# A two-layer Toeplitz mixer on Trainium2: the buffer of q * v packed densely, small tables loaded through GpSimd's queue, and the second layer's matrices written later

## The chip, the cores and the metric

The kernel runs on one core of one Trainium2 chip. The metric is device time in microseconds (us), lower is better. Before the change three runs took 6179.19, 6186.65 and 6196.39 us; the median is 6186.65 us. One further execution was taken with the hardware profiler; it took 6175.88 us, and every figure called "the trace" comes from it.

## The reference, cut to what matters

The whole network has four layers over an image batch of 8 x 56 x 56 x 192. The change touches only what the first two, of one kind, share. Each of these two computes, for every sample and channel (D1 is 576),

```
q = silu(x @ q_w.T + q_b);  v = silu(x @ v_w.T + v_b);  p = silu(x @ p_w.T + p_b)
decay = sl ** distance                        # per channel, sl from the layer's slope
a1, a2 = mlp(position) * decay                # two tables of 111 numbers per channel
qv = q * v
o1 = toeplitz along the image's width  of qv with a1
o2 = toeplitz along the image's height of qv with a2
out = (p * (o1 + o2)) @ o_w.T + o_b           # x = x + out
```

A Toeplitz product of length 56 is a multiplication by a 56 x 56 matrix whose rows are shifted copies of the table, one such matrix for each channel and direction.

## The kernel before, in words

All of it is float32. The work of the first two layers goes through four kinds of steps, and memory on the chip's outside (HBM) carries the data between them.

**q * v (`tno_qv`, lines 218 to 357).** Tiles of 128 tokens of two pairs of samples are multiplied with the q and v weights (line 257; the first four tiles of the first layer at line 278), get a bias (266, 285), silu (295) and the product (298). Three transfers for each tile, for 8, 8 and 2 *half blocks* of 32 channels, write the product to `qv` on SyncE's queue (line 301). `qv` has 18 half blocks. Each holds 64 x 56 rows of 128 numbers, of which the image fills the first 56 x 56 (T is 3136); the last 8 x 56 rows are padding, which one transfer for each of the two buffers fills with zeros at the start (line 720, on GpSimd's queue).

**The tables (`decay_tables`, from line 129).** For each layer, 18 small loads (slope and MLP weights, lines 133 to 166), a small MLP on TensorE and VectorE, and ten stores of finished tables to HBM (line 193). All 28 transfers of a layer are on SyncE's queue. A buffer `a` of a table has two copies; GpSimd clears its last column (line 182) once the transfer before has landed.

**The matrices (`expand_tables`, line 195).** 36 transfers for each layer, HBM to HBM, write `mat` from the tables: each copies 64 x 32 runs of 56 numbers (224 bytes) that start one element apart (line 201). Both layers' matrices, 72 transfers, are made during the first q * v pass of layer 0.

**The Toeplitz products (`tno_toeplitz`, from line 359).** Nine blocks of 64 channels, and for each block two directions: 18 steps n in one stage. A step loads q (`load`) and its matrices into `tm` (line 382), multiplies (`along`, line 394), and turns the result back with transposes (`turned`, line 411). For direction d = 0, `load` issues two transfers of 56 x 56 runs of 512 bytes (line 372). For d = 1 it issues one transfer: 128 partitions of 28,672 bytes (line 375). The q tile has two buffers, and the load for step n + 2 is issued when `along` of step n is done. In `along` only rows 0 to 55 of each 64 are multiplied, so the eight padding rows are loaded and never used. Sums go to HBM from GpSimd's queue (line 427).

**The output projection (`tno_out`, from line 463)** loads the sums (line 487) and x (line 114) on SyncE's queue, gates them with p, projects, and stores x on GpSimd's queue (line 117).

`tno_layers` (from line 670) sets the order. `weave` runs one "lane" of q * v or projection steps and pulls steps from another generator between them. Lane 0 is the first q * v pass with the table and matrix work beside it; it is placed by a scheduler that orders every engine's instructions by estimated times. Lanes 1 to 4 each carry a Toeplitz stage (`TZ`) among their q * v and projection steps; there TensorE, ScalarE and VectorE keep the order in which they are written, and only the two queues of transfers (SyncE's and GpSimd's) are still placed by estimate. SyncE's queue is one sequence: a transfer whose wait isn't over holds up all behind it. In the built program each of its transfers also uses one of eight semaphores in turn, and waits for the transfer eight places before it to land; GpSimd's queue has eight of its own.

Of the kernel before, what the change touches and what calls it, by code (L numbers as in the profile page):

```python
# [12 lines left out]
F32 = mybir.dt.float32  # L13
# [8 lines left out]
B, H, W, C = 8, 56, 56, 192  # L22
T = H * W
# [3 lines left out]
D1 = 576  # L27
# [6 lines left out]
def view(ap, offset, dims):  # L34

    return bass.AP(ap.tensor, ap.offset + offset, [ap.ap[0], *dims])


class Net:
# [89 lines left out]
    def decay_tables(self, L, p, tables):  # L129

        nc, inp = self.nc, self.inp
        tv = p.tile([32, 111], F32, name="tv", bufs=1)
        nc.sync.dma_start(tv, inp["tvec"])
        pows = []
        for c in range(5):
            m = min(128, D1 - 128 * c)
            sl = p.tile([128, 1], F32, name="sl")
            nc.sync.dma_start(sl[:m], inp[f"{L}_slope"][128 * c : 128 * c + m, :])
            nc.vector.tensor_scalar(sl[:m], sl[:m], 0.0, 1.0, ALU.max, ALU.min)
            nc.vector.tensor_scalar(sl[:m], sl[:m], 1.0 - 0.95, 0.95, ALU.mult, ALU.add)  # L140
            pw = p.tile([128, 64], F32, name="pw", bufs=5)
            nc.gpsimd.memset(pw[:m, 0:1], 1.0)
            n = 1
            while n < 64:
                nc.vector.tensor_scalar(
                    pw[:m, n : 2 * n], pw[:m, 0:n], sl[:m], None, ALU.mult
                )
                n *= 2
                if n < 64:
                    sq = p.tile([128, 1], F32, name="sl")  # L150
                    nc.vector.tensor_mul(sq[:m], sl[:m], sl[:m])
                    sl = sq
            pows.append(pw)
        for d in range(2):
            t = f"{L}_t{d + 1}"
            w0 = p.tile([32, 2], F32, name="w0")
            nc.sync.dma_start(w0[:, 0:1], inp[f"{t}_w0"])
            nc.sync.dma_start(w0[:, 1:2], inp[f"{t}_b0"])
            ws = p.tile([32, 3, 32], F32, name="ws")
            nc.sync.dma_start(ws, inp[f"{t}_ws"])  # L160
            bs = p.tile([32, 3], F32, name="bs")
            nc.sync.dma_start(bs, inp[f"{t}_bs"])
            wo = p.tile([32, D1], F32, name="wo")
            nc.sync.dma_start(wo, inp[f"{t}_wo"])
            bo = p.tile([128, 5], F32, name="bo")
            nc.sync.dma_start(bo, inp[f"{t}_bo"])
            h = p.tile([32, 111], F32, name="h")
            nc.vector.tensor_scalar(h, tv, w0[:, 0:1], w0[:, 1:2], ALU.mult, ALU.add)
            nc.vector.tensor_scalar(h, h, 0.0, None, ALU.max)
            for i in range(3):  # L170
                hp = self.bank2()[:32, 0, :111]
                nc.tensor.matmul(hp, ws[:, i, :], h, start=True, stop=True)
                h = p.tile([32, 111], F32, name="h")
                nc.vector.tensor_scalar(h, hp, bs[:, i : i + 1], 0.0, ALU.add, ALU.max)
            for c in range(5):
                m = min(128, D1 - 128 * c)
                ap = self.bank2()[:, 0, :111]
                nc.tensor.matmul(
                    ap[:m], wo[:, 128 * c : 128 * c + m], h, start=True, stop=True
                )  # L180
                a = p.tile([128, 112], F32, name="a")
                nc.gpsimd.memset(a[:m, 111:112], 0.0)
                back = view(pows[c][:m], 55, [[-1, 55]])
                for lo, hi, dec in ((0, 55, back), (55, 111, pows[c][:m, 0:56])):
                    nc.vector.scalar_tensor_tensor(
                        view(a[:m], 110 - lo, [[-1, hi - lo]]),
                        ap[:m, lo:hi],
                        bo[:m, c : c + 1],
                        dec,
                        ALU.add,  # L190
                        ALU.mult,
                    )
                nc.sync.dma_start(tables[d][128 * c : 128 * c + m, :], a[:m])

    def expand_tables(self, tables, mats):

# [21 lines left out]
    def tno_qv(self, L, j0, xs, gn, qv, apart=None):  # L218
# [3 lines left out]
        nc, p, inp = self.nc, self.tp, self.inp  # L222
# [5 lines left out]
        w, bias = self.wq[:, 0:2], self.wq[:, 2]  # L228
# [62 lines left out]
        def multiply(m, n, z, at, c0):  # L291
            k = n // 128
            for f in stores:
                f()
            nc.scalar.activation(z[:m, :n, :], z[:m, :n, :], AF.Silu)  # L295
            prod = p.tile([128, 4, DC * 4], F32, name="t4")
            half = z[:m, :n, :].rearrange("p (n h c) b -> p n h (c b)", h=2, c=DC)
            nc.vector.tensor_mul(prod[:m, :k], half[:, :, 0], half[:, :, 1])  # L298
            n0 = c0 // 128
            stores[:] = [  # L300
                lambda: nc.sync.dma_start(
                    qv[2 * n0 : 2 * n0 + 2 * k, at : at + m, :].rearrange("n t e -> t n e"),
                    prod[:m, :k].rearrange("p n (h e) -> p (n h) e", h=2),
                )
            ]
# [7 lines left out]
        if apart:  # L313
            units = []
            for g in range(2):
                x, t0, n = loaded[g]
                for s in range(0, n, 128):
                    for c0 in range(0, 2 * D1, 512):
                        k = min(512, 2 * D1 - c0)
# [19 lines left out]
        for g in range(2 if apart else 0, groups):  # L339
            x, t0, n = loaded.pop(0)  # L340
            for s in range(0, n, 128):
                m = min(128, n - s)
                for c0 in range(0, 2 * D1, 512):
                    k = min(512, 2 * D1 - c0)
# [14 lines left out]
    def tno_toeplitz(self, j0, mats, qv, o):  # L359
# [3 lines left out]
        nc, p = self.nc, self.tz  # L363
        PR = H // 2

        def load(n):
            blk, d = divmod(n, 2)
            q = p.tile([128, H, 128], F32, name="q", bufs=2)
            if d == 0:
                for half in range(2):  # L370
                    of = qv[2 * blk + half, :T].rearrange("(h w) e -> w h e", w=W)
                    nc.sync.dma_start(q[64 * half : 64 * half + W], of)
            else:
                of = qv[2 * blk : 2 * blk + 2].rearrange("n (h w) e -> (n h) (w e)", w=W)
                nc.sync.dma_start(q.rearrange("p i e -> p (i e)"), of)
            return q

# [59 lines left out]
        for n in range(NS):  # L437
            blk, d = divmod(n, 2)
# [220 lines left out]
            pass  # L659

    @staticmethod
    def part(gen, t):

        for dt in gen:
            yield dt
            t -= dt
            if t <= 0:
                return

    def tno_layers(self, x0, x1, x2, gn, last):  # L670


        tc, nc = self.tc, self.nc
        LS = ("L0", "L1")
        tables = [

            [self.dram.tile([D1 + 1, 112], F32, name=f"{L}_tab{d}") for d in range(2)]
            for L in LS
        ]
# [3 lines left out]
        ]  # L683
        qvs = {

            j0: self.dram.tile([D1 // 32, 64 * W, 128], F32, name=f"qv{j0}") for j0 in (0, 2)
        }
        o = [self.dram.tile([B // 2, 9, 128, T], F32, name=f"{L}_sum") for L in LS]
        x = (x0, x1, x2)
        with ExitStack() as ctx, ExitStack() as wqp:  # L690
# [5 lines left out]
            QT, OT, TZT = 25 * 2.25 * 5.3, 28 * 10.7, 8 + 72 * 3.2  # L696

            with tc.tile_pool(name="tab", bufs=2) as tab:
                stats = [self.input_stats(x0, gn[0], j, tab) for j in range(4)]
                for more in stats[0]:  # L700
                    pass
                first = Q(0, 0, tab)
                next(first)

                for n in range(14):
                    next(first)
                    next(stats[1], None)
                for more in stats[1]:
                    pass
                for n in range(10):  # L710
                    next(first)
                self.decay_tables("L0", tab, tables[0])
                for st in stats[2:]:
                    for more in st:
                        next(first)
                none = tab.tile([112, 512], F32, name="none", bufs=1)
                nc.gpsimd.memset(none, 0.0)
                for qv in qvs.values():
                    to = qv[:, T:].rearrange("n (p k) e -> p n (k e)", p=112)
                    nc.gpsimd.dma_start(to, view(none, 0, [[0, D1 // 32], [1, 512]]))  # L720
                self.decay_tables("L1", tab, tables[1])
                for t in tables:
                    for d in range(2):
                        nc.gpsimd.dma_start(t[d][D1:], none[:1, :112])
                lanes = [[(first, QT - 104.0)], [(Q(0, 2), QT)], [(O(0, 0), OT), (Q(1, 0), QT)]]
                lanes += [[(O(0, 2), OT), (Q(1, 2), QT)], [(O(1, 0), OT)], [(O(1, 2, False), OT)]]
                mat = (m for i in range(2) for m in self.expand_tables(tables[i], mats[i]))
                self.weave(lanes[0], mat, lanes[1][0][0], 72.0, 0.0, 0.88)
            in_order = tc.manual_schedule(engines=ENGINES)
            with tc.tile_pool(name="tz", bufs=1) as self.tz, in_order:  # L730
                self.tms = []
# [909 lines left out]
```

## Time and profile before

| What | Value |
|---|---|
| median of three runs | 6186.65 us |
| profiled execution, its own time / its span | 6175.88 us / 6173.9 us |
| TensorE matmuls busy | 5692.9 us (92%), 68704 instructions |
| VectorE / ScalarE / GpSimd busy | 46% / 35% / 10% |
| granted TensorE clock, mean | 0.96 |
| SyncE's queue (q1), GpSimd's queue (q0) | 909.05 MB, 54.6% / 200.98 MB, 10.4% of 16 DMA engines |
| first matmul of lane 0's q * v, first of the q * v proper (line 257) | 52.94 us, 140.14 us |
| first and last Toeplitz matmul of the four stages (lines 394, 411) | 508 to 1072, 1156 to 1983, 2095 to 2928, 3015 to 3605 us |

How to read it: the span is the stretch that the profiler covers, and the execution's own time is 2 us longer. An engine is "busy" while it executes. "DMA share" is the mean busy share of the core's 16 DMA engines; a transfer is cut into packets, and the trace records each packet's start, size and duration. Packets of one engine can overlap, so that a share may pass 1. The trace also records each increment that a DMA engine makes to a semaphore when its part of a transfer has landed. A row of the view by stretches gives, for each engine, busy us and the number of instructions, and at its end the granted clock, the DMA share and the GB/s.

### The profile page before, as it was taken

To read this page: it belongs to the slowest core of one execution; us is meant where nothing else is said; L and a number is where in the kernel's file an instruction comes from. 1 tells how busy PE (TensorE), PEld (TensorE's weight loads), DVE (VectorE), ACT (ScalarE), POOL (GpSimd) and SP (SyncE) were. 2 spreads that over 40 slices of the span, in tenths; PEclk is the share of its full clock that TensorE was granted. 3 is DMA by queue.
4 is the path that set the end of the run, shared out by engine and by line. 5 is a ranking of instruction groups with operands and counts; after the bars stand their busy time and mean duration, and the time that the engine had idled before them with its cause. 6 is when DMAs were issued, how large, how long until landed. Compare 5 with 4: busy or idle time off the path is not lost.

```text
span 6173.9 us, 151657 instructions
## 1 busy us (share of the span) xinstructions
PE 5692.9 (92%) x68704; PEld 4463.1 (72%) x68704; DVE 2845.8 (46%) x4862; ACT 2154.4 (35%) x2738; POOL 639.2 (10%) x833
## 2 busy tenths in 40 slices
PE   5998989899999999999899989999999999988998
PEld 3777878788778788778778878885565444666666
DVE  6555555444555444556444443242222322555555
ACT  2334444223444323344333332224323433333332
POOL 0000000000000000000010010000000100333332
PEclk9999999999999999999999999999999999999998
DMA  7799997888676788776899856563444322444442
GB/s 261 168 225 250 268 239 213 230 230 238 187 205 183 194 240 245 183 208 180 218 250 252 260 171 235 211 218 123 158 166 133 96 63 61 72 87 96 89 91 58
DMA packets 1139557, 1119.74 MB, mean 181 GB/s; under 512 B 342529, under 2 KB 1076737, under 8 KB 1123489
## 3 DMA queue, kind: packets, MB, share of 16 engines
q1 hardware_dynamic: 1103328, 909.05, 54.6%
q0 software_dynamic: 35584, 200.98, 10.4%
q8 instruction: 540, 8.85, 0.6%
q14 instruction: 105, 0.85, 0.0%
HBM read 753.79 MB, written 389.15 MB: 185 GB/s over the span
## 4 chain that ended last, share of the span: by engine, by line
PE 74%; DVE 10%; DMA 7%; ACT 4%; issue 3%; POOL 2%; SPq 1%; DVEq 0%; POOLq 0%; ACTq 0%
PE bank L257 15%; PE bank L394 7%; PE bank L958 6%; PE bank L511 6%; PE bank L521 5%; PE bank L411 5%; PE bank L819 5%; PE bank L1038 4%; DMA qv<-t 3%; PE bank L526 3%; PE bank L543 3%; PE bank L1052 3%; PE bank L1179 1%; DVE t L266 1%; POOL e L1284 1%
## 5 line engine op out<-in xcount | busy, mean ns | idle before, releaser
L257 PE MATMUL bank<-wq,t 128*128 128x256 f32 (+4 forms) x7680 | 1278.0, 373 | 35.0 <-DVE t L266 12.5
L257 PEld LDWEIGHTS bank<-wq,t 128*128 128x128 f32 (+2 forms) x7680 | 1005.4, 190 | 278.5 <-issue 113.0
L295 ACT ACTIVATE t<-t 128x2048 f32<-128x2048 f32 (+2 forms) x288 | 427.7, 1489 | 758.1 <-DVE t L266 752.1
L401 ACT COPY ot<-bank 128x896 f32<-128x896 f32 x576 | 484.3, 921 | 410.3 <-PE bank L394 399.7
L266 DVE TENSOR_TENSOR t<-bank,wq 128x1024 f32<-128x1024 f32 (+3 forms) x480 | 517.9, 1111 | 207.7 <-PE bank L257 205.6
L394 PE MATMUL bank<-q,tm 56*64 56x112 f32 x18432 | 524.3, 266 | 78.4 <-issue 51.0
L394 PEld LDWEIGHTS bank<-q,tm 56*64 56x64 f32 x18432 | 483.8, 138 | 113.5 <-issue 82.8
L555 ACT ACTIVATE t<-bank,wo 128x448 f32<-128x448 f32 x448 | 247.6, 634 | 887.4 <-PE bank L526 863.4
L411 PE MATMUL bank<-ident,ot 120*128 120x120 f32 x4032 | 483.2, 279 | 73.2 <-ACT ot L401 39.3
L298 DVE TENSOR_TENSOR t<-t 128x1024 f32<-128x1024 f32 (+2 forms) x288 | 274.2, 955 | 588.2 <-ACT t L295 461.4
L411 PEld LDWEIGHTS bank<-ident,ot 120*128 120x128 f32 x4032 | 441.8, 147 | 122.1 <-ACT ot L401 44.9
L511 PE MATMUL bank<-t,wo 128*128 128x224 f32 x1792 | 387.8, 371 | 45.9 <-DVE t L493 43.8
L958 PE MATMUL bank<-z,w 128*128 128x448 f32 (+1 forms) x1344 | 413.6, 555 | 2.0 <-ACT h L967 2.0
L565 DVE SCALAR_TENSOR_TENSOR t<-bank,wo,t 128x448 f32<-128x448 f32 x112 | 76.4, 682 | 699.6 <-PE bank L550 698.9
L511 PEld LDWEIGHTS bank<-t,wo 128*128 128x128 f32 x1792 | 345.9, 199 | 63.6 <-issue 40.4
L521 PE MATMUL bank<-t,wo 128*128 128x224 f32 x1792 | 362.0, 355 | 12.0 <-issue 7.2
L582 DVE TENSOR_TENSOR t<-t,t 128x896 f32<-128x896 f32 x224 | 235.6, 1082 | 296.2 <-ACT t L555 296.2
L521 PEld LDWEIGHTS bank<-t,wo 128*128 128x128 f32 x1792 | 338.8, 191 | 20.1 <-issue 13.8
L819 PEld LDWEIGHTS bank<-xt,cm 113*112 113x112 f32 x3072 | 310.7, 178 | 36.6 <-issue 30.8
L958 PEld LDWEIGHTS bank<-z,w 128*128 128x128 f32 (+1 forms) x1344 | 182.4, 189 | 205.7 <-issue 197.4
L427 POOL DMA_DIRECT2D L_sum<-s x288 | 141.0, 496 | 1757.0 <-DVE s L417 1754.5
L819 PE MATMUL bank<-xt,cm 113*112 113x108 f32 (+2 forms) x3072 | 319.0, 264 | 4.0 <-ACT h L967 2.9
(147 smaller groups left out, 7075.1 us busy)
## 6 DMA issues: line engine op xcount, KB each, us to landing
q<-qv SPq DMA_DIRECT2D x36, 3584.0 KB
q<-qv SPq DMA_DIRECT2D x72, 1568.0 KB
L_sum<-s POOLq DMA_DIRECT2D x288, 392.0 KB, 7.5
t<-L_sum SPq DMA_DIRECT2D x112, 1008.0 KB
qv<-t SPq DMA_DIRECT2D x192, 512.0 KB
cm<-in_L_cm SPq DMA_DIRECT2D x96, 896.0 KB
tm<-L_mat SPq DMA_DIRECT2D x72, 896.0 KB
x<-t POOLq DMA_DIRECT2D x112, 336.0 KB, 5.4
```

The costliest lines, as they stand in the source:

```text
L257: nc.tensor.matmul(pp[:m, b, 256 * j : 256 * j + k], x[rows, j, 2 if part else b, s : s + m], w[rows, part, c0 + c : c0 + c + k],  start=p ...
L266: nc.vector.tensor_add(z[:m, c : c + k, :], view(pp[:m], 0, [[1, k], [256, 4]]), view(bias[:m], c0 + c, [[1, k], [0, 4]]),)
L295: nc.scalar.activation(z[:m, :n, :], z[:m, :n, :], AF.Silu)
L298: nc.vector.tensor_mul(prod[:m, :k], half[:, :, 0], half[:, :, 1])
L394: nc.tensor.matmul(pt[64 * s : 64 * s + 64, r, j * 112 : (j + 1) * 112], tm[rows, c * H : c * H + 64], q[rows, PR * s : PR * s + PR, 4 * c ...
L401: nc.scalar.copy(view(ot, 4 * g, [[112 * 32, 2], [32, 112], [1, 4]]), view(pt, 0, [[512, 2], [1, 112], [112, 4]]),)
L411: nc.tensor.transpose(pz[:, i, :120], ot[:120, at : at + 128], self.ident[:120, :120])
L511: mm(gs[c // 2][:, b, c % 2 * 256 : c % 2 * 256 + N], pw[:, 0, 128 * c : 128 * c + 128], xn[:, b], start=c % 2 == 0, stop=False,)
L521: mm(P[:, b, :N], ow[:, c, 0:128], g[:, 4 * b + c], start=c == 0, stop=False)
L555: nc.scalar.activation(pg[:, c], view(gs[i], c * 256, [[512, 2], [1, N]]), AF.Silu, bias=pb[:, 2 * i + c : 2 * i + c + 1],)
L819: nc.tensor.matmul(pc[:, 128 * e + 4 * m0 : 128 * e + 4 * m1], cm[:113, e, k, :], xt[:, m0 - 1 + k : m1 - 1 + k, c + e, :], start=n == 0 a ...
L958: nc.tensor.matmul(phs[c][:, s, :TT], w0[rows, part, at : at + 128], z[rows, Z[2 if part else s], :], start=part == flip, stop=part != flip,)
```

## The change

There are three parts. The buffer `qv` loses its padding: half blocks follow each other every 56 x 56 rows, with 8 x 56 rows only after the last; the zero fill shrinks to these. The stores and both loads get new access patterns for it. The loads that reach past a half block now take the next one's first rows, which `along` doesn't use either. The tables' 28 transfers of each layer move from SyncE's queue to GpSimd's. And the second layer's 36 matrices leave lane 0: `beside` issues two of them at each step of the projection O(0, 0) in lane 2, as the text is written.

```diff
@@ decay_tables
-        nc.sync.dma_start(tv, inp["tvec"])
+        nc.gpsimd.dma_start(tv, inp["tvec"])
...
-            nc.sync.dma_start(sl[:m], inp[f"{L}_slope"][128 * c : 128 * c + m, :])
+            nc.gpsimd.dma_start(sl[:m], inp[f"{L}_slope"][128 * c : 128 * c + m, :])
...
-            nc.sync.dma_start(wo, inp[f"{t}_wo"])
+            nc.gpsimd.dma_start(wo, inp[f"{t}_wo"])
...
-                nc.sync.dma_start(tables[d][128 * c : 128 * c + m, :], a[:m])
+                nc.gpsimd.dma_start(tables[d][128 * c : 128 * c + m, :], a[:m])
@@ tno_qv, multiply
                 lambda: nc.sync.dma_start(
-                    qv[2 * n0 : 2 * n0 + 2 * k, at : at + m, :].rearrange("n t e -> t n e"),
+                    qv[: D1 // 32 * T]
+                    .rearrange("(n t) e -> t n e", t=T)[at : at + m, 2 * n0 : 2 * n0 + 2 * k],
                     prod[:m, :k].rearrange("p n (h e) -> p (n h) e", h=2),
                 )
@@ tno_toeplitz, load
             if d == 0:
                 for half in range(2):
-                    of = qv[2 * blk + half, :T].rearrange("(h w) e -> w h e", w=W)
+                    at = (2 * blk + half) * T
+                    of = qv[at : at + T].rearrange("(h w) e -> w h e", w=W)
                     nc.sync.dma_start(q[64 * half : 64 * half + W], of)
             else:
-                of = qv[2 * blk : 2 * blk + 2].rearrange("n (h w) e -> (n h) (w e)", w=W)
+                of = bass.AP(
+                    qv.tensor, qv.offset + 2 * blk * T * 128, [[T * 128, 2], [W * 128, 64], [1, W * 128]]
+                )
                 nc.sync.dma_start(q.rearrange("p i e -> p (i e)"), of)
@@ new
+    def beside(gen, other, n):
+
+        for dt in gen:
+            for i in range(n if dt else 0):
+                next(other, None)
+            yield dt
+        for more in other:
+            pass
@@ tno_layers
-            j0: self.dram.tile([D1 // 32, 64 * W, 128], F32, name=f"qv{j0}") for j0 in (0, 2)
+            j0: self.dram.tile([D1 // 32 * T + 8 * W, 128], F32, name=f"qv{j0}") for j0 in (0, 2)
...
-                    to = qv[:, T:].rearrange("n (p k) e -> p n (k e)", p=112)
-                    nc.gpsimd.dma_start(to, view(none, 0, [[0, D1 // 32], [1, 512]]))
+                    to = qv[D1 // 32 * T :].rearrange("(p k) e -> p (k e)", p=112)
+                    nc.gpsimd.dma_start(to, none)
...
-                mat = (m for i in range(2) for m in self.expand_tables(tables[i], mats[i]))
-                self.weave(lanes[0], mat, lanes[1][0][0], 72.0, 0.0, 0.88)
+
+                more = self.expand_tables(tables[1], mats[1])
+                lanes[2][0] = (self.beside(lanes[2][0][0], more, 2), OT)
+                mat = self.expand_tables(tables[0], mats[0])
+                self.weave(lanes[0], mat, lanes[1][0][0], 36.0, 0.0, 0.88)
```

More of the change, by code (lines that the diff above doesn't have):

```diff
@@ L156, in decay_tables @@
             w0 = p.tile([32, 2], F32, name="w0")
-            nc.sync.dma_start(w0[:, 0:1], inp[f"{t}_w0"])
-            nc.sync.dma_start(w0[:, 1:2], inp[f"{t}_b0"])
+            nc.gpsimd.dma_start(w0[:, 0:1], inp[f"{t}_w0"])
+            nc.gpsimd.dma_start(w0[:, 1:2], inp[f"{t}_b0"])
             ws = p.tile([32, 3, 32], F32, name="ws")
-            nc.sync.dma_start(ws, inp[f"{t}_ws"])
+            nc.gpsimd.dma_start(ws, inp[f"{t}_ws"])
             bs = p.tile([32, 3], F32, name="bs")
-            nc.sync.dma_start(bs, inp[f"{t}_bs"])
+            nc.gpsimd.dma_start(bs, inp[f"{t}_bs"])
             wo = p.tile([32, D1], F32, name="wo")
-            nc.sync.dma_start(wo, inp[f"{t}_wo"])
+            nc.gpsimd.dma_start(wo, inp[f"{t}_wo"])
             bo = p.tile([128, 5], F32, name="bo")
-            nc.sync.dma_start(bo, inp[f"{t}_bo"])
+            nc.gpsimd.dma_start(bo, inp[f"{t}_bo"])
             h = p.tile([32, 111], F32, name="h")
@@ L661, in part @@
     @staticmethod
+    def beside(gen, other, n):
[5 more added lines that the diff above has]
+            pass
+    @staticmethod
     def part(gen, t):
```

## The prediction, made before the changed kernel ran

> **What bounds the kernel now.** I read the span first: TensorE is busy for 92% of it, so a gain can come only from stretches where it waits. The view by stretches then shows where those are. Its columns are busy us of each engine, then granted clock, DMA share and GB/s. First the whole up to the first Toeplitz stage:
>
> ```profile
> 0.00:53.00 53.00, 5.50 (x25) 5.33 (x25) 13.56 (x31) 2.26 (x4) 5.90 (x22) 1.00 0.99 358
> 53.00:140.00 87.00, 72.75 (x248) 33.07 (x248) 78.04 (x199) 33.26 (x43) 0.68 (x7) 0.86 0.72 230
> ...
> 300.00:384.00 84.00, 83.81 (x520) 65.57 (x519) 48.56 (x48) 31.64 (x31) 0.00 (x0) 1.00 1.15 226
> 384.00:508.00 124.00, 96.38 (x548) 71.54 (x550) 59.99 (x60) 43.55 (x46) 0.00 (x0) 0.90 1.11 227
> ```
>
> TensorE does nothing for 53 us while DMA is full (0.99); it loses 124 - 96.4 = 27.6 us in the last stretch, with DMA over 1.1. What fills the first 53 us is in the DMA view of 0 to 50 us (queue, packets, MB, share):
>
> ```profile
> q1 hardware_dynamic: 5369, 9.56, 54.0%
> q0 software_dynamic: 2176, 8.26, 44.2%
> ...
> qv<-none POOLq DMA_DIRECT2D x2, 4032.0 KB
> ```
>
> All of q0's 8.26 MB is the zero fill, beside x. The last stretch is in the chain of waits from 380 to 510 us (start, length, what): stores of q * v and a matrix load that land late.
>
> ```profile
> 433.17 12.61 DMA qv<-t x2
> 449.39 12.66 DMA qv<-t x2
> 492.09 15.70 DMA tm<-L_mat
> ```
>
> Then the four Toeplitz stages, 2814 of 6174 us:
>
> ```profile
> 508.00:1072.00 564.00, 517.58 (x7294) 449.79 (x7295) 294.41 (x310) 242.18 (x268) 32.83 (x68) 0.95 0.90 243
> 1156.00:1983.00 827.00, 793.47 (x9263) 685.53 (x9260) 426.41 (x599) 309.70 (x398) 54.05 (x94) 0.97 0.75 210
> 2095.00:2928.00 833.00, 793.61 (x9258) 685.24 (x9255) 427.50 (x599) 309.38 (x398) 53.63 (x94) 0.97 0.75 208
> 3015.00:3605.00 590.00, 531.65 (x7563) 475.04 (x7560) 259.98 (x420) 187.09 (x268) 52.03 (x91) 0.95 0.87 242
> ```
>
> They are TensorE's (90 to 96%), but DMA is 75 to 90% busy as a mean over 16 engines: there is no room for a transfer that loads some engines more than others. Such a one is what I look for in the diff, and the d = 1 load is it. Before, as the queue's view has it:
>
> ```profile
> L375 SPq DMA_DIRECT2D q<-qv x36: 326/338/11010, 500.3 to 3529.6; - x36
> ```
>
> [...] a transfer runs on k engines[...]. Its increments by DMA engines, counted for each transfer: 16 where both sides begin with 128; 15 [...] for each of the 72 loads of line 372, 56 on both sides; 5 [...] for the 32 loads of line 1218, 96 on one side and 4 on the other. [...] four transfers of 0.4 KB issued behind the zero fill on GpSimd's queue took 40.3 us to land.
>
> **The change, part by part** (against the profiled execution's 6175.9 us; the median of the runs is 10.8 us higher).
>
> 1. *The d = 1 load.* Before, half blocks of 64 x 56 rows follow each other, so the pattern merges to 128 rows of 28,672 bytes on both sides: k = 16. Now half blocks are 56 x 56 rows apart and 64 rows are read from each; in the built program the memory side is [2][64][7168] and the tile side [128][7168]. The slowest dimensions are 2 and 128, so k = 2. The trace has the packet: 4608 of 28,672 bytes (36 x 128), median 1.062 us, about half of them within 1 ns of it and none markedly shorter, so I take it as an engine's own pace. Before, 8 on each engine: 8.5 us. Now 64 on each of two engines: 64 x 1.062 = 68.0 us.
>  What it holds up: everything issued later on SyncE's queue has a sixteenth (or fourteenth) of its packets on those two engines, behind it; with eight semaphores at most seven later transfers are even issued. Stores of q * v have three product buffers, so VectorE stands at line 298 after three units, and being in order it then frees no PSUM for TensorE.
>  Cost by the two engines' time, a block: DMA share x stage / 9, less 8.5, plus 68.0.
>  Stage 1: 0.90 x 564 / 9 = 56.4, so 115.9. Stage 2: 0.75 x 827 / 9 = 68.9, so 128.4. Stage 3: 69.4, so 128.9. Stage 4: 0.87 x 590 / 9 = 57.0, so 116.5. Sum 489.7, nine blocks 4407 us, against 2814: **+1593 us**.
>  A second road: TensorE stands from the moment its buffers run out (about 25 to 30 us: three units of 8 us in stage 1; two projection steps of some 17 us in stages 2 and 3, 20 us in stage 4) until the load lands (68 plus some 5 us queued). That adds about 45 us to a block in stages 1 to 3, 35 in stage 4: 9 x 170 = 1530. The roads agree.
>  Low end: packets of one engine overlap up to a share of 1.16 (stretch 384 to 460); the other work divided by 1.16 gives 459.7 x 9 - 2814 = 1323. High end: all 36 x 68.0 = 2448 us are added whole.
> 2. *Zero fill.* 8.26 MB become 0.46 MB. 7.8 MB at the stretch's 356 GB/s are 22 us. Behind it comes VectorE's statistics and the first slopes; I take **-20** (0 to -25).
> 3. *Tables on GpSimd's queue.* 56 issues of some 0.4 us leave SyncE, where nothing urgent stood behind them; on GpSimd, at most 10% busy, they cost some 0.5 us each as line 724 does, hidden by its idleness. Behind its waits stand its own clears of `a` (line 182). VectorE waits for the slopes earlier in its order (before the first bias addition), TensorE's order is unchanged until the table matmuls, which wait for three round trips of `a` either way. L_tab<-a landed in 2.8 to 5.3 us on SyncE's queue[...]. **0** (-8 to +10).
> 4. *Second layer's matrices.* By the order of the built program they don't reach the projection: SyncE's queue issues 10 of the 36 before the first q load and 26 among stage 1's first nine q steps. A matrix is 2048 packets of 224 bytes at a median of 16 ns over 16 engines: 2.05 us. Lane 0 loses its overload: 27.6 us of waiting less some 5 for the first q load, **-23** (-10 to -30). Stage 1 gets 26 x 2.05 = **+53** if its two engines are the bound (0 if there is room).
> 5. *qv's spacing* goes from 1,835,008 to 1,605,632 bytes. [...] **0**; a sixth of the stores' 109 us a pass (56,448 packets, 31 ns, 16 engines) either way, 18 us.
>
> Sum: 1593 - 20 + 0 - 23 + 53 = +1603: 7779 in the profile's terms, **7790 us** in the median's.
>
> **The rivals.** (a) *The load keeps its 16 engines*, because the pattern is cut otherwise when it runs. Then only parts 2 to 4 count: -20, -23, and for the 26 matrices some +12, since stage 1 has a tenth of DMA time free: 6156 us, **faster**. It decides if the load lands in under the 47 to 59 us that lie, by the matmuls of line 394, between its issue and its `along` in stage 1. Against it stand the counts of 15 and 5 above. 8%. (b) *Two engines, but others pass it*: then only the chain counts, issue, 68, `along` of some 14 us and a few between, 88 us a block: +25 and +22 in stages 1 and 4, a few in 2 and 3, 9 x 53 = 480: 6620 us. Against it: the 40.3 us above. 10%. (c) *Nothing overlaps it*: 36 x 68.0 + 53 - 43: 8645 us. For it: seven transfers ahead are few, and the clock falls after stalls (0.90 against 1.00 in the first fence). 12%. My forecast has 70%.
>
> **How the numbers follow.** The low end is part 1's low end with a margin towards (b), 7300; the high end lies on the way to (c), 8450. About 0.3% is what a measurement of this kernel can tell from no change; slower by more has 0.92 (all but (a)), faster 0.06, same 0.02 from (a)'s low and high matrix price.
>
> **What would show it.** Right: 2 or 3 increments by DMA engines for each d = 1 load, landing some 70 us after issue; DMA share near 0.5 in the stages; `qv<-t` and `q<-qv` on the chain of waits; stages of about 1090, 1155, 1160 and 1050 us; TensorE starting near 33 us. Wrong: a load that lands in some 11 us, or stages as long as before.

## The result, and the profile after

The changed kernel takes 8074.45 us (median of 4 runs, 8066.58 to 8084.38), beside 6188.31 us for the kernel before on the same chip: a ratio of 1.3073, with an interval of 1.3053 to 1.3092. The prediction was 7790 us, in a range of 7300 to 8450: the sign and the place were right, and the loss was larger by some 280 us.

First the same view by stretches as for the kernel before (start and end; then busy us of PE, PEld, DVE, ACT, POOL; granted clock, DMA share, GB/s). The first two lines reach up to the first Toeplitz stage, the other four are the Toeplitz stages:

```profile
0.00:33.00 33.00, 7.63 (x27) 6.43 (x28) 17.04 (x60) 4.39 (x8) 14.11 (x40) 1.00 0.97 335
33.00:458.00 425.00, 386.73 (x2151) 280.46 (x2151) 277.56 (x465) 161.02 (x168) 25.25 (x63) 0.93 0.78 191
458.00:1555.00 1097.00, 546.54 (x7293) 475.24 (x7293) 297.04 (x313) 245.83 (x273) 32.86 (x68) 0.74 0.53 135
...
1638.00:2942.00 1304.00, 811.39 (x9261) 698.71 (x9258) 426.26 (x599) 310.16 (x398) 54.50 (x94) 0.80 0.50 137
...
3054.00:4366.00 1312.00, 815.94 (x9266) 702.16 (x9265) 426.36 (x599) 310.74 (x398) 54.55 (x94) 0.80 0.49 136
...
4452.00:5502.00 1050.00, 561.46 (x7566) 504.94 (x7562) 255.52 (x420) 187.87 (x268) 53.58 (x91) 0.75 0.49 136
```

The stages last 1097, 1304, 1312 and 1050 us where they lasted 564, 827, 833 and 590: 1949 us more. TensorE's busy time in them grows by only 100 us; the rest is standing. The DMA share falls from between 0.75 and 0.90 to about 0.5: less is in flight while the kernel waits for DMA, which is what a transfer on few engines looks like in a mean over 16.

The load itself, in the DMA view of one of them, the fourth of stage 2 (from its first to its last packet, 2029.9 to 2114.0 us, cut into 40 slices of 2.1 us: busy tenths of the 16 engines, then GB/s):

```profile
DMA  9201599793118599979951111111111111111110
GB/s 406 73 41 58 95 234 296 179 272 136 61 66 272 152 238 274 238 197 225 177 212 70 53 53 53 53 53 53 53 53 59 49 61 56 55 55 55 55 51 38
```

For its last 36 us or so the share is about 1 tenth and the rate some 55 GB/s: two engines of 16 (two packets of 28,672 bytes in 1.066 us are 53.8 GB/s). TensorE in the same block, in three stretches:

```profile
2029.90:2076.00 46.10, 45.56 (x547) 39.60 (x546) 19.53 (x35) 14.67 (x23) 6.46 (x11) 1.00 0.66 181
2076.00:2122.60 46.60, 0.54 (x3) 0.19 (x2) 1.16 (x2) 0.00 (x0) 0.00 (x0) 0.56 0.24 86
2122.60:2169.70 47.10, 45.34 (x536) 39.06 (x536) 21.98 (x40) 13.93 (x23) 2.39 (x3) 0.97 0.80 191
```

It works on for 46 us after the load's first packet, stands for 46, and goes on at 2122.6, 8.6 us after the load's last packet. What it waited for is VectorE (line 586), which waited for a load of sums (`t<-L_sum`) issued on SyncE's queue at 2052.2, behind the d = 1 load; it landed at 2121.3. Over the whole execution two groups of the page show such waits (the time after the last bar is the engine's idle time, with what ended most of it):

```profile
L298 DVE TENSOR_TENSOR t<-t 128x1024 f32<-128x1024 f32 (+2 forms) x288 | 273.9, 957 | 1556.8 <-DMA qv<-t 1158.6
...
L586 DVE TENSOR_TENSOR t<-t,t 128x896 f32<-128x896 f32 x224 | 236.2, 1087 | 1023.7 <-DMA t<-L_sum 692.5
```

Before, the first line ended with "588.2 <-ACT t L295 461.4" and the second with "296.2 <-ACT t L555 296.2". In the trace each of the 36 loads now has 3 increments (16 before). By the medians one comes 0.43 us after the load's issue ends, the other two 81.2 and 82.8 us after the issue begins, and with the last of them the load has landed; before, it landed after 13.2. Of the load's packets two are in flight in 80% of its time and more than two in 0.3%, where 16 or more were in 66%. So it runs on two engines: that is the reason that was forecast.

Stretch by stretch, so that the numbers can be set beside the experiments. Lane 0 ends here with the first matmul of `along`, and a stage is counted from the first to the last matmul of `along` (without the last transposes, so some 12 to 19 us shorter than above):

| us | lane 0 ends | stage 1 | stage 2 | stage 3 | stage 4 | four stages |
|---|---|---|---|---|---|---|
| before | 507.9 | 552 | 808 | 815 | 572 | 2746 |
| after | 457.9 | 1085 | 1285 | 1293 | 1032 | 4694 |

Lane 0 gains 50 us, the stages lose 1948, and what lies between and after them loses 11 more: 1909, the difference of the two spans (8082.6 and 6173.9).

### The profile page after: what moved, and what is told of

Read it like the earlier page. It is cut to its first block, busy times and chain, and to the rows that moved or that the text cites. A ratio compares the mean times of both kernels' runs of the same rounds, so it can differ in the third digit from the quotient of the medians.

```text
span 8082.6 us, 151644 instructions
## 1 busy us (share of the span) xinstructions
PE 5783.5 (72%) x68704; PEld 4541.5 (56%) x68704; DVE 2842.4 (35%) x4862; ACT 2158.3 (27%) x2738; POOL 670.9 (8%) x889
## 4 chain that ended last, share of the span: by engine, by line
PE 49%; another core or an unknown queue 21%; DVE 8%; DMA 7%; SPq 3%; ACT 2%; issue 2%; POOL 1%; DVEq 0%; POOLq 0%; ACTq 0%
PE bank L257 7%; PE bank L975 4%; PE bank L415 4%; PE bank L525 4%; DMA L_sum<-s 4%; PE bank L398 4%; PE bank L836 4%; PE bank L515 4%; PE bank L1055 3%; PE bank L530 2%; PE bank L1069 2%; PE bank L547 2%; DVE t L266 2%; DMA qv<-t 1%
## 5 line engine op out<-in xcount | busy, mean ns | idle before, releaser
L398 PE MATMUL bank<-q,tm 56*64 56x112 f32 x18432 | 556.8, 276 | 826.1 <-DVE t L266 489.6
L398 PEld LDWEIGHTS bank<-q,tm 56*64 56x64 f32 x18432 | 514.3, 145 | 863.1 <-DVE t L266 494.4
L415 PE MATMUL bank<-ident,ot 120*128 120x120 f32 x4032 | 502.3, 286 | 546.6 <-DVE t L266 434.1
L415 PEld LDWEIGHTS bank<-ident,ot 120*128 120x128 f32 x4032 | 460.2, 152 | 596.4 <-DVE t L266 438.1
L295 ACT ACTIVATE t<-t 128x2048 f32<-128x2048 f32 (+2 forms) x288 | 426.5, 1487 | 1377.8 <-DVE t L266 1374.3
L525 PE MATMUL bank<-t,wo 128*128 128x224 f32 x1792 | 385.4, 371 | 477.6 <-DVE t L586 468.1
L525 PEld LDWEIGHTS bank<-t,wo 128*128 128x128 f32 x1792 | 356.6, 201 | 492.9 <-issue 478.8
L515 PE MATMUL bank<-t,wo 128*128 128x224 f32 x1792 | 398.3, 378 | 86.2 <-DVE t L497 44.3
L515 PEld LDWEIGHTS bank<-t,wo 128*128 128x128 f32 x1792 | 353.7, 204 | 105.5 <-DVE s L418 43.2
L418 DVE COPY s<-bank 128x784 f32<-128x784 f32 x288 | 259.9, 966 | 239.4 <-DMA L_sum<-s 203.3
L117 POOL DMA_DIRECT2D x<-t x112 | 91.2, 814 | 2799.9 <-DVE t L572 2072.4
```

The source lines that it names most:

```text
L398: nc.tensor.matmul(pt[64 * s : 64 * s + 64, r, j * 112 : (j + 1) * 112], tm[rows, c * H : c * H + 64], q[rows, PR * s : PR * s + PR, 4 * c ...
L415: nc.tensor.transpose(pz[:, i, :120], ot[:120, at : at + 128], self.ident[:120, :120])
L418: nc.vector.tensor_copy(to, view(pz, 0, [[128, n], [64, 2], [1, 56]]))
L515: mm(gs[c // 2][:, b, c % 2 * 256 : c % 2 * 256 + N], pw[:, 0, 128 * c : 128 * c + 128], xn[:, b], start=c % 2 == 0, stop=False,)
L525: mm(P[:, b, :N], ow[:, c, 0:128], g[:, 4 * b + c], start=c == 0, stop=False)
```

## The experiments

**Which part is it, and is it the number of engines?** Four kernels took the d = 1 load as the suspect. Three of them keep it one transfer of 128 packets of 28,672 bytes and change only the number of groups in the pattern, and with it k, the prediction's number of engines. The edit, here for 8 groups:

```
-                    qv.tensor, qv.offset + 2 * blk * T * 128, [[T * 128, 2], [W * 128, 64], [1, W * 128]]
+                    qv.tensor,
+                    qv.offset + 2 * blk * T * 128,
+                    [[14 * W * 128, 8], [W * 128, 16], [1, W * 128]],
```

With 16 groups, [[7 * W * 128, 16], [W * 128, 8], ...] (in these three kernels rows reach the tile in another order; the transfer's size and the work behind it stay the same):

> The changed kernel with one edit: the d = 1 load reads 16 groups of 8 rows, the groups 7 rows apart, instead of 2 groups of 64 rows 56 apart. It stays one transfer of 128 packets of 28,672 bytes, but the slowest dimension is 16 (16 groups, 128 partitions), so k = 16. The rows reach the tile in another order (some twice, others 1 to 15 partitions lower), so its q is not the reference's. My theory (the loss is the load on two engines and nothing else): as before or a little faster, some 6145 us (lane 0 gains 40 to 50 us, the matrices in stage 1 give some of it back). Rival (a good part of the loss is the new spacing of q * v, or the matrices in stage 1, or the tables' queue): well over 6250 us. Packets: 8 an engine, landing in 11 to 13 us, 16 increments for a load.

With 8 groups:

> The changed kernel with one edit: the d = 1 load reads 8 groups of 16 rows, 14 rows apart (rows reach the tile in another order, so its q is not the reference's). k = 8: 16 packets an engine, 17 us of packets. Theory S (TensorE works on for some 27 us after the load is issued, then stands until it lands; the loss is landing time less 27 us, for each of 36 blocks): landing 20 to 26 us, no loss, 6145 to 6200 us. Theory E (the loss is the time of the loaded engines: other work 48 to 61 us a block plus the load's own share, where it is more than the block took before): stages 1 to 4 give +2, 0, 0, 0 us a block, 6145 to 6190 us. Both agree here; a theory of cost in proportion to the load's length from the first microsecond would give +8.5 us a block, 6450 us.

With 4 groups, [[28 * W * 128, 4], [W * 128, 32], ...]:

> The changed kernel with one edit: the d = 1 load reads 4 groups of 32 rows, 28 rows apart (rows reach the tile in another order, so its q is not the reference's). k = 4: 32 packets an engine, 34 us of packets. Theory S (stand from 27 us after issue until the load lands): landing 42 to 47 us, so 15 to 20 us a block, 36 blocks: +540 to +720, 6690 to 6870 us, and about as much in each of the four stages. Theory E (time of the loaded engines): +19, +3, +2, +17 us a block in stages 1 to 4, 9 x 41 = +366, 6510 us, nearly all of it in stages 1 and 4. Cost in proportion to length from the first microsecond: +26 us a block, 7070 us.

And the load as two transfers, which keeps every row in its place:

```
+                for half in range(2):
+                    at = (2 * blk + half) * T
+                    of = qv[at : at + 64 * W].rearrange("(h w) e -> h (w e)", w=W)
+                    nc.sync.dma_start(q[64 * half : 64 * half + 64].rearrange("p i e -> p (i e)"), of)
```

> The changed kernel with one edit: each d = 1 load is written as two transfers, one for each half block, 64 rows of 28,672 bytes on both sides, so k = 16 for each and 4 packets an engine. The same bytes and the same rows in the same places. My theory: the loss is gone, within 20 us of the kernel with 16 groups, some 6145 us, below the kernel before. Rival (the loss lies in other parts of the change): over 6250 us. The 36 more issues on SyncE cost nothing if SyncE is not what is late.

Measured (the load from its first packet's start to its last packet's end, its packets' duration and its landing are medians over the 36 loads; the last row is the changed kernel against its own runs of before, 6188.31):

| kernel | median, us | ratio to before | increments | packet, us | load, us | lands after, us | four stages |
|---|---|---|---|---|---|---|---|
| before | 6160.33 | | 16 | 1.06 | 10.8 | 13.2 | 2746 |
| 16 groups | 6308.13 | 1.0235 [1.0218, 1.0253] | 16 | 2.21 | 18.7 | 21.7 | 2929 |
| two transfers | 6299.76 | 1.0221 [1.0202, 1.0241] | 16 each | 2.24 | 19.1 | 19.9 each | 2909 |
| 8 groups | 6775.63 | 1.1000 [1.0975, 1.1026] | 9 | 1.95 | 37.9 | 40.6 | 3390 |
| 4 groups | 7669.66 | 1.2440 [1.2420, 1.2460] | 5 | 1.68 | 66.3 | 69.8 | 4280 |
| after, 2 groups | 8074.45 | 1.3073 [1.3053, 1.3092] | 3 | 1.07 | 78.8 | 82.8 | 4694 |

All four expectations missed, and by the same thing. The increments are 16 for k = 16, 9 for 8 and 5 for 4 (below 16 one more than k, as with the changed kernel's 3), so the loads did run on 16, 8 and 4 engines; but the load did not become shorter in proportion. From 2 engines to 4 it shrank only from 78.8 to 66.3 us, and on 16 engines it took 18.7 us where the kernel before took 10.8. A packet that took 1.06 us before took 1.7 to 2.2 us in the median of these kernels, and single ones up to 3.4 us. 3.67 MB a load make 196, 97 and 55 GB/s with 16, 8 and 4 groups, 340 in the kernel before and 47 in the changed one. A load's rate follows something else as well as k.

What that is, the runs don't show: the records don't say which partition a packet writes. They do show why 4 engines gain little: each has half the packets of one of two engines, but each packet takes 1.68 us where it took 1.07, so that the packets of an engine come to 32 x 1.68 = 54 us where they came to 64 x 1.066 = 68; the load went from 78.8 to 66.3.

One suspect for the 16 engines' slower load was the new spacing: that q * v's new distance between half blocks slows its own loads and stores. **The kernel before, with nothing changed but its d = 1 load cut in two:**

```
-                of = qv[2 * blk : 2 * blk + 2].rearrange("n (h w) e -> (n h) (w e)", w=W)
-                nc.sync.dma_start(q.rearrange("p i e -> p (i e)"), of)
+                for half in range(2):
+                    of = qv[2 * blk + half].rearrange("(h w) e -> h (w e)", w=W)
+                    nc.sync.dma_start(q[64 * half : 64 * half + 64].rearrange("p i e -> p (i e)"), of)
```

> The kernel before with one edit: each d = 1 load is two transfers of 64 rows on 64 partitions, so k = 16 for each. Theory P ([...] 64 partitions, or 16 groups of 8, took 19 us where 128 partitions in one transfer took 10.5; the rest of the loss of the two k = 16 kernels comes from this): a load takes 19 us, and the kernel loses what those two lost, about +130 to +190, 6290 to 6350 us. Rival (the spacing of q * v in memory, 1,605,632 bytes between half blocks, slows their loads or stores): here the spacing is the old one, so a load takes 10 to 11 us and the time is that of before, 6160 us.

6341.31 us, ratio 1.0266 [1.0243, 1.0288]; packets of 2.25 us, the load 18.9 us, the stages 2890: the same as with the new spacing (2909, of which 30 us are matrices, see below). One load in the view by stretches, first of this kernel and then of the kernel before (the stretch is the load's first to last packet):

```profile
1462.40:1481.50 19.10, 18.57 (x136) 16.07 (x137) 8.87 (x15) 2.97 (x6) 2.26 (x4) 1.00 1.01 223
```

```profile
1405.30:1416.30 11.00, 11.00 (x92) 9.14 (x90) 2.91 (x6) 2.66 (x5) 0.74 (x1) 1.00 1.02 418
```

The DMA share is 1.01 and 1.02, so the 16 engines are "busy" all the time in both; they are just about half as fast in the first (223 and 418 GB/s of all transfers). The busy share doesn't tell these slow packets (2.25 us) from the fast ones (1.06). The distance between half blocks is ruled out, and cutting the load at 64 partitions is shown to nearly double its time (18.9 us for 10.8). Why it does so was not shown: the cut changes both the partitions of one transfer and the rows of memory that it reads, and no kernel here changes one side alone.

**Would two queues use both halves of the partitions at once?** The changed kernel with the two transfers above, the second half on ScalarE's queue ("(nc.scalar if half else nc.sync).dma_start"). "Ring" stands in this expectation and the next for a queue's packets on one engine:

> The changed kernel with the d = 1 load as two transfers of 64 rows (k = 16 each), the first half on SyncE's queue, the second on ScalarE's. Theory P: if the two rings are worked side by side, the halves use both halves of the partitions at one time, the pair takes 9 to 12 us instead of 19 to 20, and the kernel is near 6150 us. Rival [...]: 19 us and 6300 us as with both on one queue.

6322.19 us, 1.0237 [1.0213, 1.0261]: nothing gained. The pair takes 18.4 us (median), with packets of 2.08 us; on one queue it was 19.1 us, with packets of 2.24.

**Is it the order in SyncE's queue?** The changed kernel with the load, its pattern as it was, on ScalarE's queue ("nc.scalar.dma_start(q.rearrange(...), of)"):

> The changed kernel with the d = 1 load, still one transfer on two engines, issued from ScalarE's queue. [...] Theory F (the loss is the order within SyncE's ring; an engine shares its time among rings by bytes): the stores of q * v land early, only the chain issue, load, first step counts, 6600 to 7500 us. Theory G [...]: a store of q * v has 64 packets of 512 bytes on each engine, each waits for one of 28,672 bytes (1.06 us), so it lands as late as before and the load later still: 8000 to 8500 us. Theory E (the time of the two engines is what counts): as the prediction has it, 7790 us.

8132.47 us, 1.3174 [1.3144, 1.3204]; the load takes 78.8 us and lands after 83.0, as on SyncE's queue. The time lies in theory G's range, not in F's or at E's 7790. The load's 132.12 MB are now on a queue of their own, q10 on this kernel's page. The waits are the same as in the changed kernel, on the same page:

```profile
L298 DVE TENSOR_TENSOR t<-t 128x1024 f32<-128x1024 f32 (+2 forms) x288 | 273.7, 956 | 1558.4 <-DMA qv<-t 1170.4
...
L586 DVE TENSOR_TENSOR t<-t,t 128x896 f32<-128x896 f32 x224 | 236.1, 1085 | 1160.3 <-DMA t<-L_sum 861.5
```

So a queue of its own for the load doesn't bring SyncE's transfers past it. Of those issued on SyncE's queue while a load was under way, 5 of 135 landed before the load; in the changed kernel it was none of 111. GpSimd's transfers do pass: all 278 in the changed kernel and 268 of 273 here. A store of q * v has 64 packets for each engine and landed after 74.0 us (median; 72.8 in the changed kernel); a store of sums from GpSimd's queue has two packets for each engine and landed after some 19. In which order an engine takes the packets of several queues was not measured, so the reason that theory G gives for its range is not shown.

**The other parts alone.** Tables and matrices together, q * v as before:

> The kernel before with the change's other parts: tables' transfers on GpSimd's queue and the second layer's matrices written beside lane 2; q * v, its zero fill and its loads as before. By the prediction's parts 3 and 4: 0 and -23, and some +12 for 26 matrices among stage 1 where DMA has a tenth of its time free: 6150 us; with the +53 of full engines in stage 1: 6190 us. By the trace of the changed kernel (lane 0 shorter by 50 us, 20 of it the smaller fill): -30 + 12, 6140 us.

Tables alone:

> The kernel before with the tables' transfers alone (slopes, the small weights, the tables themselves: 56) on GpSimd's queue. The zero fill keeps its 8.26 MB and stands behind them on that queue. The prediction said 0 (-8 to +10): 6170 to 6190 us. With tables and matrices together TensorE's first matmul came at 33 us instead of 56 though the fill kept its size, so theory T: the earlier start comes from the tables' move, which puts the fill later, and the fill then costs its 20 us of DMA time further on in lane 0; lane 0 ends within 10 us of before, the total within 10 us. Rival: the fill's new place is free, and the whole is 20 us shorter, 6155 us.

Matrices alone:

> The kernel before with the second layer's matrices alone beside lane 2 (by SyncE's order 26 of 36 come among stage 1's first nine q steps). The prediction said -23 in lane 0 and +53 in stage 1: 6205 us. By the run with tables and matrices (lane 0 -31, stage 1 +30): lane 0 some -25, stage 1 +30, within 10 us of before. TensorE starts at 56 us as before if theory T for the tables' move holds.

Their edits are the change's own lines. Measured (TensorE's first matmul, lane 0's end and the stages from the trace; the ratio of the last row is to its own runs of before, 6177.53):

| kernel | median, us | ratio to before | first matmul | lane 0 ends | stage 1 | stages 2 to 4 |
|---|---|---|---|---|---|---|
| before | 6173.43 | | 43.9 | 507.9 | 552 | 2195 |
| tables | 6172.38 | 0.9997 [0.9988, 1.0007] | 21.6 | 509.1 | 545 | 2179 |
| matrices | 6173.74 | 1.0005 [0.9995, 1.0015] | 43.3 | 471.0 | 590 | 2186 |
| both | 6174.42 | 0.9993 [0.9982, 1.0004] | 21.9 | 477.2 | 582 | 2188 |

None moves the time. The tables' move brings TensorE's first matmul 22 us forward and lane 0's end not at all. The zero fill is as large as before and now stands behind the tables on GpSimd's queue; that it takes its DMA time later, in a lane whose DMA share is high (0.90 from 53 to 509 us), fits this. The matrices take 37 us from lane 0 and give 38 to stage 1; the view by stretches of the kernel with the matrices alone, lane 0 and stage 1, shows the DMA share moving with them (0.77 and 0.96, where it was 0.90 in both before):

```profile
53.00:471.00 418.00, 391.40 (x2152) 284.25 (x2150) 278.27 (x493) 163.68 (x174) 5.49 (x25) 0.93 0.77 190
471.00:1074.00 603.00, 529.63 (x7299) 459.37 (x7298) 298.03 (x313) 243.85 (x271) 32.93 (x68) 0.92 0.96 249
```

**A version that beats both.** The matrices belong where DMA has room, in stage 2 (0.75). SyncE's queue doesn't keep the order as written there: in the changed kernel the matrices are written beside lane 2, and it issues 10 of the 36 in lane 0 and 26 in stage 1. TensorE, ScalarE and VectorE do keep it. So the matrices went to ScalarE's queue:

```
-                more = self.expand_tables(tables[1], mats[1])
-                lanes[2][0] = (self.beside(lanes[2][0][0], more, 2), OT)
+                more = self.expand_tables(tables[1], mats[1], nc.scalar)
...
-                for n, tz in enumerate((TZ(0, 0), TZ(0, 2), TZ(1, 0), TZ(1, 2))):
+                for n, tz in enumerate((TZ(0, 0), self.beside(TZ(0, 2), more, 1), TZ(1, 0), TZ(1, 2))):
...
-                self.nc.sync.dma_start(mat[n].rearrange("p (c w) -> p c w", w=H), src)
+                (queue or self.nc.sync).dma_start(mat[n].rearrange("p (c w) -> p c w", w=H), src)
```

> The kernel with tables' transfers on GpSimd's queue and q * v as before, and the second layer's matrices not beside lane 2 on SyncE's queue but beside the second Toeplitz stage on ScalarE's queue, whose order is kept as written: the 36 lie in the first half of stage 2. Theory: lane 0 keeps its gain of 31 us, stage 1 has no matrices and its 30 us are saved, stage 2 has DMA room (0.75 busy) and loses 0 to 10 us, so 6140 to 6150 us, faster than before by some 0.5%. Rival: the matrices cost their DMA time wherever they lie (36 x 1.2 us), 6175 us, no change.

6145.28 us, 0.9953 [0.9938, 0.9969] against before: 0.5% faster, a small gain, but the interval leaves 1 out, and so faster than both kernels. ScalarE issues the 36 matrices from 1109 to 1521 us, in the first half of stage 2. Its view by stretches, lane 0, stage 1 and stage 2:

```profile
33.00:472.00 439.00, 390.61 (x2152) 283.02 (x2152) 277.93 (x481) 165.05 (x176) 26.00 (x64) 0.92 0.73 191
472.00:1035.00 563.00, 516.01 (x7297) 446.93 (x7296) 296.14 (x312) 242.72 (x271) 32.95 (x68) 0.96 0.90 243
1120.00:1953.00 833.00, 795.68 (x9262) 685.84 (x9255) 429.44 (x599) 310.26 (x398) 53.58 (x94) 0.97 0.82 228
```

Lane 0 keeps 36 us of gain, stage 1 is as long as before (563 us, 564 then), and stage 2, whose DMA share rises from 0.75 to 0.82, is some 6 us longer.

## Why the prediction was right in kind and 280 us short

**Two engines, by the pattern's slowest dimension: right.** 3 increments for each of 36 loads; and 9, 5 and 16 with 8, 4 and 16 groups. (Of the 15, 5 and 3 increments in the traces of the two kernels one comes within 0.6 us of the issue's end, ahead of any landing.) By the slowest dimensions of the two sides, the engines (increments without that one) were 16 for 128 and 128, 14 for 56 and 56, 4 for 96 and 4, and 16, 8, 4 and 2 for 128 with 16, 8, 4 and 2 groups. Before the changed kernel ran, the first three alone were measured; k = 2 was the author's estimate.

**64 packets of 1.062 us, 68 us: right for the packets, short for the load.** They measured 1.066 us. But from first to last packet the load took 78.8 us, and it landed 82.8 us after its issue began; the prediction had 68 plus some 5. Two of its packets are in flight in 80% of the 78.8 us, one in 17% and none in 3%, and GpSimd's transfers land while the load is under way.

**The cost of a block by the two engines' time: the step that failed.** The prediction took 115.9, 128.4, 128.9 and 116.5 us from it; the stages' stretches give 122, 145, 146 and 117 (a ninth of each). In stages 1 and 4 the sum is right to the us (with stage 1's 53 us for the matrices, of which 30 to 38 were measured). Between the end of one load and the start of the next the DMA share is 0.95 and 0.94 there, so the engines do fill their time; but the second road, below, gives nearly the same, and these runs don't tell the two apart in stages 1 and 4. In stages 2 and 3, where TensorE and not DMA had been the bound, it assumed that TensorE's work and the load would overlap up to the engines' full time. They don't: the buffers run out long before the load lands, and between the loads the share is only 0.73. Stages 2 and 3 are 17 us a block short, some 300 us: the whole error.

**The second road, TensorE stands until the load lands: right in kind, and it should have been used for all four.** Per block, means of nine, from the trace (TensorE's time between the load's first and last packet, and outside; the stages as in the first view):

| us a block | load lasts | busy in it | stands in it | stands outside it | stood before the change | longer busy | more in all |
|---|---|---|---|---|---|---|---|
| stage 1 | 77.1 | 27.1 | 50.0 | 11.2 | 5.2 | 3.2 | 59 |
| stage 2 | 78.6 | 33.0 | 45.6 | 9.2 | 3.7 | 2.0 | 53 |
| stage 3 | 78.6 | 33.4 | 45.2 | 9.9 | 4.4 | 2.4 | 53 |
| stage 4 | 82.3 | 34.2 | 48.1 | 6.2 | 6.5 | 3.3 | 51 |

The cover of "25 to 30 us" was 27 to 34, and the standing of "some 45" in stages 2 and 3 is 45. What that road lacked: 5 us in stage 1 (a load of 77 us with a cover of 27); some 6 us more of standing outside the load in stages 1 to 3 (in the block shown above TensorE goes on 8.6 us after the load's last packet); 13 us in stage 4 (it had 35 there; the load lasts 82 us and the cover is 34); and 2 to 3 us of longer busy time, at a granted clock of 0.74 to 0.80 where it had been 0.95 to 0.97. Its 170 us for the four blocks came to 216.

The experiments support the form. Taking the stages' 2746 us and, where the matrices were moved, 30 us for them in stage 1 (582 less 552), the loss of a block is (four stages - 2776) / 36: 4.3, 17.1, 41.8 and 53.3 us for loads of 18.7, 37.9, 66.3 and 78.8. The load's length less the loss is 14, 21, 24.5 and 25.5 us: beyond some 25 us nearly every us of the load is lost, no matter whether it sits on 2 engines or on 4.

**Rival (a), 16 engines kept, 6156 us, "faster": its price was wrong.** The rival as worked out assumed 8.5 us of packets. With 16 engines in the new spacing no pattern tried here gave that; the three that were tried give 6300, 6308 and 6322 us, slower than before. Its sign rested on the pattern being cut as before, to 128 rows of one pitch, and the new spacing has no such pitch.

**Rivals (b) and (c).** (b) needs SyncE's transfers to pass the load; with the load on a queue of its own 5 of 135 do (8132 us). (c), nothing overlaps, has 68 us a block in its sum where 51 to 59 were lost: a cover of 27 to 34 us exists.

**Zero fill, -20: about right in size, though its mark was another's.** Lane 0 ends at 458 to 464 us in the seven kernels with the small fill and both other parts, and at 477 and 472 in the two with the large fill (tables and matrices together, and the matrices on ScalarE's queue): some 14 us, in which the new spacing of q * v's stores is contained too. But "TensorE starting near 33 us" is not the fill's mark. The first matmul of q * v came at 52.9 before, at 35.5 with the tables alone, fill unchanged, and at 30.8 in the changed kernel: 17 of these 22 us are the tables', and they are worth nothing.

**Tables, 0: right** (0.9997); the 20 stores of tables had landed in 1.5 to 5.3 us, though, not in 2.8 to 5.3. **Matrices, -23 and +53: mis-sized,** -37 and +38, so together nothing rather than +30; the 2.05 us a matrix were too dear in stage 1: 38 / 26 = 1.5 alone, and 30 / 26 = 1.2 with the tables. **Spacing, 0: right as far as shown,** by the two kernels with the load cut in two: their stages last 2909 - 30 = 2879 us with the new spacing and 2890 with the old.

## What to carry to other kernels

When a layout loses its padding, look at how the transfers that read it merge: a pitch that no longer fits can take a load from 128 uniform rows to [2][64], and with it 14 of 16 DMA engines (the load took 10.8 us before and 78.8 after). Cost such a load by its landing time less what the buffers cover, and count a stage's DMA share as room only for work that TensorE isn't made to wait for; and when repairing it, look at the packets' durations and not at the number of engines alone, since 16 engines on 64 partitions took nearly twice as long as on 128 (18.9 us and 10.8). Work moved off a stretch with a high DMA share gained nothing here where it landed in another such stretch, and gained some 30 us where it landed in one with room, on a queue whose order was kept.

## What the runs showed that was not expected

- The same 128 packets of 28,672 bytes took 1.06 us each on 16 engines over 128 partitions, 2.2 us on 16 engines over 64 partitions or in 16 groups of 8, and 1.07 us on two engines.
- A load on 4 engines (66.3 us) was hardly shorter than on 2 (78.8 us).
- The DMA share doesn't show this: 1.01 in a load with 223 GB/s in flight, 1.02 in one with 418.
- A separate queue for a slow transfer freed nothing (83.0 us to land, 8132 us), nor did two queues for two halves (18.4 us, 18.9 to 19.1 on one). GpSimd's stores of two packets for each engine landed after some 19 us and passed the slow load, SyncE's of 64 after 72.8 and did not (none of 111 of its transfers did).
